# A two-layer graph network: two edits in the hand-written order of the first two groups (norm sums, and two statistics of the next x)

## The chip, the cores and the metric

The kernel runs on one core of one Trainium2 chip. The metric is the device time of one execution in microseconds (us); lower is better. Engines are called by the names of the profile: PE (TensorE, matrix products), PEld (its weight loads), DVE (VectorE), ACT (ScalarE), POOL (GpSimd) and SP (which only issues transfers).

## The reference, cut to what matters

The input x is 128 batches of 128 x 512, float32; adj is 128 x 128.

```python
# layer 0
h = jnp.maximum(_layernorm(x, axis=-1), 0.0)
q, k, v = (einsum('bnd,ed->bne', h, W) for W in (Wq, Wk, Wv))
rel = adj.T[None] * einsum('bnd,bmd->bnm', q, k)
rel = rel / jnp.linalg.norm(rel, axis=2, keepdims=True)
x = x + einsum('bnm,bmd->bnd', rel, v)
# layer 1
h = jnp.maximum(_layernorm(x, axis=-1), 0.0)
q, k, v = h @ Wq + bq, h @ Wk + bk, h @ Wv + bv      # 8 heads of 64
scores = q k^T / sqrt(64) + where(adj == 0, -1e9, 0)
x = x + softmax(scores) v
```

## The kernel before, in words

The 128 batches are worked in 32 groups of four (G = 4). One group of a layer is a matrix of 512 x 512, so a projection is a 512 x 512 x 512 product. It is made by a scheme with seven block products instead of eight (`Product`, L206 to L266). Its methods P1 to P7 each issue eight matmuls on PE into one PSUM bank (called x, y or z) and then either copy the bank into a quarter of the result on ACT (P1, P4, P5, P6: L232 or L235) or add the bank to a quarter on DVE (P2, P3, P7: L248). The bank x is used four times in turn, by P1, P6, P7 and P4: P6, P7 and P4 go on adding to what is there. So P4 may write only when P7's addition has read the bank.

For layer 0, q and k are folded into one matrix (`G`, the product with the folded weights; its result is gT), and `V` is the value product, with result v. P2 adds to the quarter of batches 0 and 1 and columns 0 to 255, P3 to batches 0 and 1 and columns 256 to 511, P7 to batches 2 and 3 and columns 256 to 511; P4 gives batches 2 and 3, columns 0 to 255.

The steps of layer 0 around the change are:
- `stat(b)` (L285): mean and variance of batch b of x, two DVE instructions (L289, L290); `inv(i)` (L292): four small instructions, which turn the statistics of two batches into scale and shift. In layer 0 all four are on POOL, in layer 1 the first two on DVE.
- `hn(i)` normalizes two batches on ACT (L308) and sends them to DRAM in blocks; `rd(i)` fetches them back (L197, SP); `T(i)` turns them on DVE (L320) into half i of h. h in this turned form feeds the products. `sumA` and `sumB` (L363 to L368) are the sums of blocks that the products need.
- `R` (L391, PE): the scores; `mask_rel` (L400, DVE) multiplies them with adj and gives rel; `square` (L406, ACT) gives the squares sq.
- `norms` (L408): turns sq (L412), and sums it in one reduction (L415), three small copies (L419) and four small reductions (L422), nine instructions on DVE; then one power on POOL gives rn (L427).
- `O(b)` (L431, PE): rel times v for one batch; `xO(b)` (L437, DVE): x becomes x + rn times that. Its batch of v must be whole by then.

Layer 1 has the products Q, K and V, the scores `S` (L476), the masking and maximum per row (`mkA`, `mkB`: L546 and L549; `add_mask`, `mx`: L488 and L493), the exponentials on ACT (`exC`, `exD`, `ex`: L529 and L500), a turn of the weights through DRAM (`wr`, `wt`), and the product with v (`A`, L632).

All five engines run under a manual schedule: on each engine the instructions stand in the order in which the program issues them, and each engine takes its own from the front, waiting where an operand is not ready. That order is written out by hand as lists of steps, which `run` plays. A step is named by who and what: m is layer 0 of this group, l layer 1 of the group before, p of the one before that, f layer 0 of the group after, and n is layer 1 of this group. `FIRST` is played once, for group 0; `SECOND` once, for group 1; `ORDER` for groups 2 to 31; `LAST` at the end. A step such as m.V.P3 issues its PE and its DVE instructions both, and so fixes their place in two queues.

In `ORDER` the four statistics of f and the two inversions stand together ahead of m.V.P6, and m.norms stands directly behind m.square.

Of the kernel before, what the change touches and what calls it, by code (L numbers as in the profile page):

```python
# [21 lines left out]
def kernel(  # L22
# [350 lines left out]
    class Layer0(Layer):  # L373
        n = 0
# [64 lines left out]
    class Layer1(Layer):  # L439
        n = 1  # L440
# [230 lines left out]
    FIRST = """  # L671
        m.sumA m.sumB m.start f.stat0 f.stat1 f.inv0 m.G.P1 m.G.P2 f.stat2 f.stat3 f.inv1 w.sumw m.G.P5 f.hn0 f.rd0 m.G.P6
        w.scale m.G.P3 m.V.P1 f.hn1 f.rd1 w.sumv m.G.P7 m.V.P2 w.sumq m.G.P4 m.V.P5
        m.R m.mask_rel m.square f.T0 m.V.P6 m.V.P3 m.norms m.V.P7 m.O0 m.xO0 m.O1 m.xO1 n.stat0 n.stat1
        n.inv0 m.V.P4 n.hn0 n.rd0 f.T1 f.start f.G.P1 f.sumA m.O2 m.xO2 m.O3 m.xO3 n.stat2 n.stat3 n.inv1
        f.G.P5 f.sumB f.G.P6 n.hn1 n.rd1 f.G.P2 f.G.P3 f.G.P7 n.T0 f.G.P4 w.sumk n.T1 n.start
    """.split()
    SECOND = """
        l.Q.P1 l.sumA l.Q.P2 l.sumB l.K.P1 l.K.P2 l.Q.P5 l.Q.P6 l.sto0 l.sto1 f.load0 f.load1 l.Q.P3 l.K.P5 l.K.P6 l.Q.P7
        l.K.P3 l.K.P7 f.load2 f.load3 l.Q.P4 l.K.P4 m.V.P1 f.stat0 f.stat1 f.inv0  # L680
        m.V.P2 m.V.P6 m.R m.mask_rel m.square m.norms f.stat2 f.stat3 f.inv1
        l.S0 l.S1 l.mkA1 m.V.P5 l.exC1 l.mkB1 m.V.P7 l.exD1 l.wr1 l.add_mask0 m.V.P3 l.mx0
        m.V.P4 l.ex0 l.wr0 m.O0 m.xO0 m.O1 m.xO1 n.stat0 n.stat1 n.inv0 n.hn0 n.rd0 l.start_v l.V.P1 m.O2 m.xO2 m.O3 m.xO3
        n.stat2 n.stat3 n.inv1 l.V.P2 l.V.P5 n.hn1 n.rd1 l.wt1 l.V.P6
# [33 lines left out]
    with tc.manual_schedule(engines={EN.PE, EN.SP, EN.Pool, EN.DVE, EN.Activation}):  # L718
        o, p, l, m = None, None, None, Layer0(0)
# [9 lines left out]
        f = Layer0(1)  # L729
# [3 lines left out]
        for g in range(NG):  # L733
            n = Layer1(g)
            if g:
                f = Layer0(g + 1) if g + 1 < NG else None
            run((FIRST, SECOND, ORDER)[min(g, 2)], o=o, p=p, l=l, m=m, n=n, f=f, w=Weights1())
            o, p, l, m = p, l, n, f
# [31 lines left out]
```

## Time and profile before

| | us |
|---|---|
| median of three runs | 2467.14 |
| the three runs | 2465.93 to 2468.3 |
| the profiled execution, its own time | 2463.63 |
| its span, first to last instruction | 2461.8 |
| PE busy | 2449.3 |
| DVE busy | 1756.1 |
| ACT busy | 1014.5 |
| POOL busy | 377.0 |

The granted TensorE clock was 0.999 on average. The chain of work that ended last lists stretches in order of time; in the stretch behind group 1 it goes from one PE step to the next. Times within the span are counted from its start: group 0's scores R run from about 39 to 43 us, those of group 1 from 97 to 101 us, and a later group takes about 76 us. A timeline row gives start, duration, engine, line, operation, the tiles it writes and reads, and, where the engine was idle before it, for how long and what ended that. A row of the waits gives the total, the number and the longest.

### The profile page before, as it was taken

How to read it: one execution, taken by the hardware profiler on the slowest of the kernel's cores; microseconds unless marked ns; L12 is line 12 of the kernel's file. 1: busy time of each engine (PE TensorE's matmuls, PEld its weight loads, DVE VectorE, ACT ScalarE, POOL GpSimd, SP SyncE). 2: the span in 40 equal slices, each digit the busy share in tenths (PEclk: the TensorE clock that was granted, in tenths of full speed). 3: DMA queues.
4: the chain of work that ended last, by engine and by line, in shares of the span. 5: the costliest groups of instructions: out<-in, count | busy, mean ns of one | idle time of the engine just before them, and what ended most of it. 6: DMA issues, size and time to landing. Idle time of an engine off the chain costs nothing.

```text
span 2461.8 us, 40194 instructions
## 1 busy us (share of the span) xinstructions
PE 2449.3 (99%) x14432; PEld 2111.2 (86%) x14432; DVE 1756.1 (71%) x2994; ACT 1014.5 (41%) x3248; POOL 377.0 (15%) x692
## 2 busy tenths in 40 slices
PE   9999999999999999999999999999999999999998
PEld 7888888888888888888888888888888888888887
DVE  6567776677767677776777667776767776677767
ACT  3334433444434344343443344443434434344434
POOL 5110111111111111111011111111111111111111
PEclk9999999999999999999999999999999999999999
DMA  5357656677566775566766667756677566676656
GB/s 189 99 164 206 178 166 178 172 204 198 161 174 171 189 214 161 163 182 180 206 178 170 175 171 204 196 162 174 172 190 213 162 170 174 180 205 186 165 156 163
DMA packets 396407, 438.18 MB, mean 178 GB/s; under 512 B 31600, under 2 KB 289008, under 8 KB 396208
## 3 DMA queue, kind: packets, MB, share of 16 engines
q1 hardware_dynamic: 297376, 201.22, 32.7%
q10 hardware_dynamic: 70000, 165.96, 18.2%
q0 software_dynamic: 28832, 68.44, 13.5%
q8 instruction: 114, 1.87, 0.3%
q14 instruction: 85, 0.70, 0.1%
HBM read 204.80 MB, written 230.69 MB: 177 GB/s over the span
## 4 chain that ended last, share of the span: by engine, by line
PE 96%; DVE 2%; DMA 1%; issue 0%; SPq 0%; POOL 0%; ACT 0%; DVEq 0%; POOLq 0%
PE pv_x L224 17%; PE pg_x L224 9%; PE pk_x L224 9%; PE pq_x L224 9%; PE pv_z L224 9%; PE pr L391 5%; PE po L632 5%; PE pq_z L224 5%; PE pg_z L224 5%; PE pk_z L224 4%; PE pv_y L224 4%; PE po L431 4%; PE pss L476 3%; PE pg_y L224 2%; PE pso L476 2%; PE pq_y L224 2%
## 5 line engine op out<-in xcount | busy, mean ns | idle before, releaser
L320 DVE STREAM_TRANSPOSE h<-u_h 128x1024 f32<-128x1024 f32 x126 | 156.6, 1243 | 215.7 <-DMA u_h<-d_h 214.9
L224 PE MATMUL pv_x<-wc_v,h 128*128 128x256 f32 x1280 | 306.1, 382 | 3.7 <-DVE v L248 2.7
L224 PEld LDWEIGHTS pv_x<-wc_v,h 128*128 128x128 f32 x1280 | 240.2, 190 | 55.3 <-issue 21.6
L666 POOL DMA_DIRECT2D out_dram<-o x124 | 110.7, 900 | 982.8 <-DVE o L659 939.2
L308 ACT ACTIVATE hn<-xb,shift,rstd 128x512 f32<-128x512 f32 x252 | 191.2, 807 | 149.7 <-POOL shift L300 122.1
L224 PE MATMUL pv_z<-wc_v,s 128*128 128x256 f32 x1024 | 245.2, 382 | 0.8 <-DVE v L241 0.8
L224 PEld LDWEIGHTS pv_z<-wc_v,s 128*128 128x128 f32 x1024 | 191.9, 190 | 29.8 <-DVE v L241 1.2
L232 ACT COPY gT<-pg_x 128x512 f32<-128x512 f32 x96 | 56.3, 586 | 364.0 <-PE pg_x L224 363.1
L224 PE MATMUL pq_x<-h,wc_q 128*128 128x256 f32 x768 | 181.6, 379 | 0.4 <-DVE h L320 0.2
L529 ACT ACTIVATE e<-pso,nmax 128x128 f32<-128x128 f32 x504 | 179.6, 393 | 5.5 <-DVE nmax L549 5.4
L224 PE MATMUL pv_x<-wc_v,s 128*128 128x256 f32 x768 | 181.5, 379 | 0.0
L224 PE MATMUL pk_x<-h,wc_k 128*128 128x256 f32 x768 | 181.5, 379 | 0.0
L289 DVE BATCH_NORM_STATS2 st<-xb 128x6 f32<-128x512 f32 x256 | 171.4, 669 | 8.2 <-DMA xb<-in_x_dram 8.1
L515 DVE STREAM_TRANSPOSE wT<-u_w 128x1024 f32<-128x1024 f32 x126 | 152.4, 1210 | 32.8 <-DMA u_w<-d_w 32.2
L224 PEld LDWEIGHTS pq_x<-h,wc_q 128*128 128x128 f32 x768 | 145.7, 190 | 20.9 <-PE pv_x L224 1.1
L224 PEld LDWEIGHTS pk_x<-h,wc_k 128*128 128x128 f32 x768 | 145.8, 190 | 20.0 <-issue 0.2
L224 PEld LDWEIGHTS pv_x<-wc_v,s 128*128 128x128 f32 x768 | 145.8, 190 | 19.9
L643 ACT COPY oT<-po 128x512 f32<-128x512 f32 x124 | 72.1, 582 | 206.3 <-PE po L632 203.9
L299 POOL TENSOR_TENSOR rstd<-rstd,mhalf 128x2 f32<-128x2 f32 x128 | 91.0, 711 | 408.0 <-DVE shift L298 408.0
L70 POOL DMA_DIRECT2D xb<-in_x_dram x124 | 69.0, 557 | 436.6 <-DMA out_dram<-xb 246.2
L232 ACT COPY v<-pv_x 128x512 f32<-128x512 f32 x96 | 56.3, 586 | 178.7 <-PE pv_x L224 178.7
L224 PE MATMUL pg_z<-s,wc_a 128*128 128x256 f32 x512 | 121.3, 380 | 0.8 <-ACT v L232 0.6
(153 smaller groups left out, 4906.0 us busy)
## 6 DMA issues: line engine op xcount, KB each, us to landing
d_h<-hn ACTq DMA_DIRECT2D x126, 512.0 KB, 3.8
u_h<-d_h SPq DMA_DIRECT2D x504, 128.0 KB, 3.7
d_w<-e ACTq DMA_DIRECT2D x126, 512.0 KB, 3.3
u_w<-d_w SPq DMA_DIRECT2D x504, 128.0 KB, 3.3
out_dram<-xb SPq DMA_DIRECT2D x126, 256.0 KB, 3.9
xb<-in_x_dram POOLq DMA_DIRECT2D x124, 256.0 KB, 4.7
d_o<-oT ACTq DMA_DIRECT2D x62, 512.0 KB, 2.8
u_o<-d_o SPq DMA_DIRECT2D x248, 128.0 KB, 4.0
```

The lines of the kernel that those rows point to most:

```text
L224: nc.tensor.matmul(ps[:, m, :], lhsT=lhsT, rhs=rhs, start=first and m == 0 and k == 0, stop=k == 1, skip_group_check=True,)
L232: nc.scalar.copy(to, ps)
L289: nc.vector.bn_stats(st, x_tiles[g, b])
L308: nc.scalar.activation(hn[:, r], x_tiles[g, b].rearrange("p (k j q) -> p j k q", j=TB, q=BK), AF.Relu, bias=self.shift[:, b : b + 1], scal ...
L320: nc.vector.transpose(half.rearrange("p k (t i) -> p t k i", i=BK), self.u.pop(i).rearrange("p t (k q) -> p t k q", q=BK),)
L391: nc.tensor.matmul(pr[:, b, :], lhsT=self.turned(k, b), rhs=self.gT[k // 2][:, k % 2, ts(b, P)], start=(k == 0), stop=(k == KD - 1),)
L431: nc.tensor.matmul(po, lhsT=self.rel[:, b, :], rhs=self.v[:, b, :], start=True, stop=True)
L476: nc.tensor.matmul(half[r][:, k, :], lhsT=self.qT[rows, k, ts(b, P)], rhs=self.kT[rows, k, ts(b, P)], start=True, stop=True,)
L515: nc.vector.transpose(self.wT[b].rearrange("p h (t i) -> p t h i", i=BK), self.uw.pop(b).rearrange("p t (h q) -> p t h q", q=BK),)
L529: nc.scalar.activation(e[:, :, i, :], sc[:, k, :].rearrange("p (j q) -> p j q", q=BK), AF.Exp, bias=nmax[:, i : i + 1], accum_out=self.tot ...
L632: nc.tensor.matmul(po[r * HD : (r + 1) * HD, k, :], lhsT=self.v[b // 2][:, b % 2, ts(2 * k + r, HD)], rhs=wT[:, r * NH + k, :], start=True ...
L666: nc.gpsimd.dma_start(out[g * G + b], o.rearrange("p k t q -> p (k t q)"), accum_op=ALU.add)
```

## The change

Two places in the written order. In `FIRST`, m.norms moves from behind m.V.P3 to behind f.T0, ahead of m.V.P6 and m.V.P3. In `SECOND`, f.stat2, f.stat3 and f.inv1 move from behind m.norms to ahead of m.V.P6, and with that ahead of m.R, m.mask_rel, m.square and m.norms. No step is added or taken away, and the lists `ORDER` and `LAST` stay as they are.

```diff
     FIRST = """
...
-        m.R m.mask_rel m.square f.T0 m.V.P6 m.V.P3 m.norms m.V.P7 m.O0 m.xO0 m.O1 m.xO1 n.stat0 n.stat1
+        m.R m.mask_rel m.square f.T0 m.norms m.V.P6 m.V.P3 m.V.P7 m.O0 m.xO0 m.O1 m.xO1 n.stat0 n.stat1
...
     SECOND = """
...
         l.K.P3 l.K.P7 f.load2 f.load3 l.Q.P4 l.K.P4 m.V.P1 f.stat0 f.stat1 f.inv0
-        m.V.P2 m.V.P6 m.R m.mask_rel m.square m.norms f.stat2 f.stat3 f.inv1
+        m.V.P2 f.stat2 f.stat3 f.inv1 m.V.P6 m.R m.mask_rel m.square m.norms
         l.S0 l.S1 l.mkA1 m.V.P5 l.exC1 l.mkB1 m.V.P7 l.exD1 l.wr1 l.add_mask0 m.V.P3 l.mx0
```

## The prediction

> **What bounds the kernel now.** I read the page first: busy shares, then the shares of the chain that ended last.
>
> ```profile
> span 2461.8 us, 40194 instructions
> ...
> PE 2449.3 (99%) x14432; PEld 2111.2 (86%) x14432; DVE 1756.1 (71%) x2994; ACT 1014.5 (41%) x3248; POOL 377.0 (15%) x692
> ...
> PE 96%; DVE 2%; DMA 1%; issue 0%; SPq 0%; POOL 0%; ACT 0%; DVEq 0%; POOLq 0%
> ```
>
> TensorE (PE) is busy for all but 2461.8 - 2449.3 = 12.5 us, and 96% of the chain is PE. An edit to another engine's order can only win time by removing a place where PE stands still. The next view is therefore who waited for whom, for PE alone (total, times, longest):
>
> ```profile
> PE pv_x L224 <- DVE v L248: 2.7, 2, 1.8
> ...
> PE pq_x L224 <- DVE h L320: 0.2, 1, 0.2
> ```
>
> The largest entry is two waits of V's product for L248, the DVE addition of a finished product into the tile v. They lie in the two groups that the diff touches. PE's timeline shows the first (start, us, engine, line, tiles, idle before it):
>
> ```profile
> 44.41 1.89 PE L224 MATMUL pv_z<-wc_v,s 128*128 128x256 f32 x8
> 46.13 1.89 PE L224 MATMUL pv_x<-wc_v,s 128*128 128x256 f32 x8
> 47.86 1.88 PE L431 MATMUL po<-v,rel 128*128 128x512 f32 x4
> 50.61 1.96 PE L224 MATMUL pv_x<-wc_v,h 128*128 128x256 f32 x8 [0.87 <-DVE v L248]
> ```
>
> These are V.P3, V.P7, O0 with O1, and V.P4. V.P4 writes into the bank that V.P7's addition reads, so it waits for that addition. DVE's timeline of the same time says why the addition was late:
>
> ```profile
> 43.49 1.23 DVE L320 STREAM_TRANSPOSE h<-u_h 128x1024 f32<-128x1024 f32 x1
> 46.40 0.69 DVE L248 TENSOR_TENSOR v<-pv_z,v 128x512 f32<-128x512 f32 x1 [1.68 <-PE pv_z L224]
> 47.01 0.70 DVE L412 STREAM_TRANSPOSE sqt<-sq 128x512 f32<-128x512 f32 x1
> ...
> 49.77 0.69 DVE L248 TENSOR_TENSOR v<-pv_x,v 128x512 f32<-128x512 f32 x1
> ```
>
> V.P7's addition could have run at about 48.12 (V.P3's starts 46.40 - 44.41 = 1.99 after its matmuls, and 46.13 + 1.99 = 48.12), but the norm sums (47.01 to 49.77) stood ahead of it. Before 46.40 DVE was idle for 1.68 us, although the squares (ACT, 43.60 + 0.63) were ready at 44.23. The second group, DVE and then PE:
>
> ```profile
> 104.95 0.69 DVE L289 BATCH_NORM_STATS2 st<-xb 128x6 f32<-128x512 f32 x1
> ...
> 106.58 0.67 DVE L546 TENSOR_TENSOR pso<-pso,mask 128x512 f32<-128x512 f32 x1
> ...
> 109.22 0.68 DVE L248 TENSOR_TENSOR v<-pv_x,v 128x512 f32<-128x512 f32 x1
> ```
> ```profile
> 106.23 1.89 PE L224 MATMUL pv_z<-wc_v,s 128*128 128x256 f32 x8
> 109.96 1.99 PE L224 MATMUL pv_x<-wc_v,h 128*128 128x256 f32 x8 [1.84 <-DVE v L248]
> ```
>
> From 102.19 on DVE has no gap until V.P7's addition at 109.22, and two statistics of the next x lie in that run (104.95 to 106.58, 1.63 us). Ahead of it, between 96.26 and 100.80, DVE is idle.
>
> **What these places cost.** I count from start to start, since the ends of matmuls are modelled. One product step takes 1.73 us where nothing waits, O0 with O1 1.72 (115.46 to 117.18 in the chain). Group 0: 47.86 to 50.61 is 2.75, so 1.03 too long, and V.P4 behind it takes 1.80, 0.07 too long. A second wait follows: O2 with O3 starts at 54.13, G.P5 at 56.16, which is 2.03, 0.31 too long, and the product behind it 1.83, 0.10 too long; the chain has sumA (L363, 55.41 to 56.10) just before it, itself at the end of an unbroken DVE run from xO0 on. Together 1.51 us. Group 1: 106.23 to 109.96 is 3.73, 2.00 too long, and 0.10 behind it: 2.10 us.
>
> **Part 1, group 0.** Nothing is added or removed; nine DVE instructions move ahead of one (V.P3's addition) and POOL's rn starts earlier. The order built from the changed code has PE, ACT and SP as before; no DMA is moved.
> - The norms start behind the transpose f.T0. An independent instruction starts 1.16 after such a transpose (65.70 to 66.86), so at 43.49 + 1.16 = 44.65. They take 2.76 (47.01 to 49.77): V.P3's addition starts at 47.41 instead of 46.40, and ends at 48.10.
> - This is the new wait. O0 reads the half of v that V.P3's addition writes; PE would be there at 47.86 and starts 0.06 after the addition's end (as at 109.90 to 109.96): 48.16. Late by 0.30, and some 0.08 behind it. Behind O0 on PE stand O1 and everything else.
> - V.P7's addition follows at about 48.1 and ends at 48.8. V.P4 is due at 48.16 + 1.72 + 0.07 = 49.95 and waits no longer.
> - rn (POOL, 1.01) ends at about 48.5. xO0 needs O0, 1.19 after its start (111.79 to 112.98): 49.35 instead of 50.86. The second follows at 50.15 and the statistics at about 50.8 instead of 52.19, 1.37 earlier. The run behind moves with them: sumA ends at 54.73. G.P5 is due at 49.95 + 3 x 1.73 = 55.13 (V.P4, G.P1, O2 with O3): the 0.31 goes too.
> - Next late is G.P4 at 65.84 behind G.P7's own addition (65.10); it hangs on PE alone and stays. n.T0's last landing (63.89, start 65.70) leaves 1.8 us, Q.P5 behind n.T1 has 1.9 us (72.59 to 74.58).
>
> Gain 1.51 - 0.38 = **1.13 us**. Bounds: 0.63, if the wait at G.P5 stays (0.41) and the hand-over takes 0.15 as at 50.46 to 50.61; 1.51, if O0 did not wait at all.
>
> POOL's rn comes beside V.P3's and V.P7's additions. Today it stands beside V.P7's (49.82 and 49.77), which takes 0.69 as elsewhere; but DVE L90 takes 1.75 beside POOL L90 (39.31 and 38.81), against 0.69 at 21.41 with POOL only issuing DMAs. I take nothing. The Trainium skill, "SBUF — State Buffer", section "Who interferes with whom", says that DVE and GpSimd share ports which the first holds for its whole instruction, but not against a DVE instruction with a single SBUF input, as these additions have; the trace agrees. If the lock held here all the same, V.P7's addition would come some 1 us later, at about 49.1, and the sum would lose 0.1 at most, an estimate by that page.
>
> **Part 2, group 1.** Four DVE instructions (two statistics of 0.69 and 0.66, two aggregations of 0.18) move from 104.95 to behind V.P2's addition, 96.3 to 97.9, in the 4.54 us in which DVE waits for the scores R. Their x landed at 78.3. POOL's four small instructions (inv1) move with them into idle time, ahead of rn. V.P7's addition starts at 109.22 - 1.63 = 107.59; its matmuls (104.51 + 1.99) and the scores (PE, 101.69 + 1.06) are ready. V.P4 starts at 108.33 instead of 109.96; free of waits it would be 107.96, so 0.37 stays. V.P3's addition and the exponentials keep their distance and move up alike; ACT and the transfers d_w, u_w, d_h, u_h follow. Gain **1.63 us**. Upper bound 2.10, the whole wait; lower bound 0.53: that is how far ahead n.T0 (ends 130.93) is of Q.P1 (131.46), and if its data did not come earlier, the rest would be given back there.
>
> **Sum.** 1.13 + 1.63 = 2.76 us. The profiled execution took 2463.63 us (span 2461.8): 2460.9 after. It lies 3.5 us below the median of the runs, 2467.14, from which 2464.4 follows. That is my forecast: 0.11%, less than the 0.2% (4.9 us) that I take as what a measurement of this kernel can tell from no change.
>
> **Rivals.**
> 1. *One gain is given back*: n.T0 does not move up with PE (group 1 yields 0.53), or group 0 only 0.63. For it: 281.67 and following show PE held at Q.P1 by a transpose that waited for its DMA, 283.06 - 280.92 = 2.14 against 1.83. Against: in both groups what feeds the transfers hangs on O0 to O3, which move up. Time: 2467.14 - 1.16 = 2466.0.
> 2. *Slower*: the later groups meet their transfers differently. Place: the boundary of groups, where n.T0 waits for u_h. In two of the 30 later groups PE loses there today, 0.31 at 283.06 and 0.30 at 290.35, and alike at 1116.64 and 1123.93: 0.61 a group. With five more such groups the gain is gone (2.76 / 0.61 = 4.5), and with the 28 others all hit the time is 2464.4 + 17.1 = 2481.5. Against: 76 us a group is PE's own pace, the transfers are released by work behind PE, and so they should shift as one.
> 3. *More than the stalls' length*, if PE ran slowly behind a gap. By rows: 16 matmuls (two steps, 3.46 us) at half speed behind each of the two long gaps would add 6.9 us, so 2457.5. Against: behind 50.90 and 110.28 the matmuls follow at 0.216 as anywhere, and the granted clock of both stretches is 1.00. The Trainium skill, "TensorE: Matmul & The Clock Gate", section "What's actually happening", gives such a halving after an idle window of about 3.4 us; the gaps here are shorter, and the trace agrees.
>
> That the change does not do what it says is ruled out by the built order.
>
> **Numbers.** Forecast 0.84, rival 1 0.10, rival 2 0.04, rival 3 0.02. The profiled execution shows that one can fall 3.5 us below the median, so 0.05 of the forecast lies below 2462.2. Faster by over 0.2%: 0.05 + 0.02 = 0.07; within: 0.79 + 0.10 = 0.89; slower: 0.04. Range: the profiled execution's own sum, 2460.9, is the low end; the high end is the smallest gain (1.16) with the runs' spread upward (1.2) and some room for rival 2: 2467.8.
>
> **What would show it.** Right: no wait of V.P4 in group 0, a new one of about 0.3 of po (L431) for L248; in group 1 a wait of about 0.2 instead of 1.84; PE's busy time unchanged and the span 2.8 shorter, with everything behind 131 earlier by 2.8. Wrong: G.P5 still late, Q.P1 waiting for L320, or steps of over 1.83 us at later boundaries.

## The result, and the profile after

| | before | after |
|---|---|---|
| median, 17 runs each | 2467.14 us | 2462.55 us |
| lowest to highest | 2464.55 to 2470.38 | 2460.41 to 2466.47 |
| ratio after to before | | 0.9984, 95% interval 0.9977 to 0.9991 |
| profiled execution, own time | 2463.63 | 2460.41 |
| its span | 2461.8 | 2458.6 |

The changed kernel is faster by 0.16%, and the interval (2.2 to 5.7 us) excludes no change. The forecast, 2.76 us less, lies in it. The medians lie 4.6 us apart, so the measured one is 1.9 us below 2464.4. With 17 runs each, this settles a change smaller than the 0.2% that the prediction took as the limit.

The page after, the same rows:

```profile
span 2458.6 us, 40193 instructions
...
PE 2450.2 (100%) x14432; PEld 2111.9 (86%) x14432; DVE 1756.6 (71%) x2994; ACT 1012.7 (41%) x3248; POOL 375.9 (15%) x692
...
PE 92%; DVE 4%; DMA 2%; issue 1%; SPq 0%; ACT 0%; POOL 0%; DVEq 0%; ACTq 0%; POOLq 0%
```

No engine's work changed (PE busy 2449.3 and 2450.2); PE's idle time went from 12.5 to 8.4 us. The waits of PE:

```profile
PE idle L121 <- POOL ident masks.py:199: 1.4, 1, 1.4
PE pg_x L224 <- DVE gT L248: 0.8, 1, 0.8
PE pv_x L224 <- DVE v L241: 0.5, 1, 0.5
PE pq_x L224 <- DVE h L320: 0.3, 2, 0.2
```

The entry of 2.7 us for V's product and L248 is gone. PE in group 0 (V.P6, V.P3, V.P7, O0 with O1, V.P4, G.P1, O2 with O3, and the first half of G.P5):

```profile
43.80 1.89 PE L224 MATMUL pv_x<-wc_v,s 128*128 128x256 f32 x8
45.52 1.89 PE L224 MATMUL pv_z<-wc_v,s 128*128 128x256 f32 x8
47.25 1.89 PE L224 MATMUL pv_x<-wc_v,s 128*128 128x256 f32 x8
49.23 1.98 PE L431 MATMUL po<-v,rel 128*128 128x512 f32 x4
51.05 1.89 PE L224 MATMUL pv_x<-wc_v,h 128*128 128x256 f32 x8
52.78 1.89 PE L224 MATMUL pg_x<-h,wc_a 128*128 128x256 f32 x8
54.51 1.88 PE L431 MATMUL po<-v,rel 128*128 128x512 f32 x4
56.22 1.03 PE L224 MATMUL pg_z<-s,wc_a 128*128 128x256 f32 x4
```

This execution happens to be 1.12 us late already at V.P6 (43.80 against 42.68; in the kernels below, equal up to here, the same step starts anywhere from 42.81 to 44.15), so steps must be read as differences. O0 now comes 1.98 after V.P7 instead of 1.73: the new wait, 0.25 us, which the list of waits does not have because the modelled end of V.P7's matmuls (47.25 + 1.89) covers most of it. V.P4 comes 1.82 after O0 instead of 2.75, and the row has no idle time any more. G.P5 comes 1.71 after O2 with O3 instead of 2.03. DVE shows the reason (T0, the first of the norms, V.P3's addition, V.P7's addition, xO):

```profile
44.60 1.24 DVE L320 STREAM_TRANSPOSE h<-u_h 128x1024 f32<-128x1024 f32 x1
45.76 0.67 DVE L412 STREAM_TRANSPOSE sqt<-sq 128x512 f32<-128x512 f32 x1
...
48.48 0.69 DVE L248 TENSOR_TENSOR v<-pv_z,v 128x512 f32<-128x512 f32 x1
49.18 0.69 DVE L248 TENSOR_TENSOR v<-pv_x,v 128x512 f32<-128x512 f32 x1
50.47 1.53 DVE L437 SCALAR_TENSOR_TENSOR xb<-po,rn,xb 128x512 f32<-128x512 f32 x2 [0.60 <-PE po L431]
```

The norms follow T0 after 1.16 and take 2.72. V.P3's addition ends at 49.17 and O0 starts 0.06 later. In group 1, DVE's first row below is V.P2's addition, then come the two statistics in what was idle time, and the run of masks and maxima no longer holds them; the second fence is PE's V.P5, and behind V.P7 its V.P3, V.P4 and O0:

```profile
95.53 0.69 DVE L248 TENSOR_TENSOR v<-pv_y,v 128x512 f32<-128x512 f32 x1 [4.67 <-PE pv_y L224]
96.14 0.68 DVE L289 BATCH_NORM_STATS2 st<-xb 128x6 f32<-128x512 f32 x1
...
100.76 0.69 DVE L400 TENSOR_TENSOR rel<-pr,adj_sb 128x512 f32<-128x512 f32 x1 [2.92 <-PE pr L391]
...
107.46 0.68 DVE L248 TENSOR_TENSOR v<-pv_x,v 128x512 f32<-128x512 f32 x1
```
```profile
102.63 1.99 PE L224 MATMUL pv_z<-wc_v,s 128*128 128x256 f32 x8
...
106.19 1.89 PE L224 MATMUL pv_z<-wc_v,s 128*128 128x256 f32 x8
108.19 1.99 PE L224 MATMUL pv_x<-wc_v,h 128*128 128x256 f32 x8
110.02 1.94 PE L431 MATMUL po<-v,rel 128*128 128x512 f32 x4
```

V.P4 comes 2.00 after V.P3, was 3.73. DVE's idle time ahead of the scores shrank from 4.54 to 2.92, by the 1.62 that the statistics take.

To compare executions I take two lengths from PE's starts: group 0 from V.P6 to Q.P1, and group 1 from V.P5 to O0. In the kernel before, these four steps are:

```profile
42.68 1.89 PE L224 MATMUL pv_x<-wc_v,s 128*128 128x256 f32 x8
67.67 1.89 PE L224 MATMUL pq_x<-h,wc_q 128*128 128x256 f32 x8
102.67 1.99 PE L224 MATMUL pv_z<-wc_v,s 128*128 128x256 f32 x8
111.79 1.95 PE L431 MATMUL po<-v,rel 128*128 128x512 f32 x4
```

Before: 67.67 - 42.68 = 24.99 and 111.79 - 102.67 = 9.12. After: 67.63 - 43.80 = 23.83 and 110.02 - 102.63 = 7.39. That is **1.16 + 1.73 = 2.89 us**, against a forecast of 1.13 + 1.63 = 2.76.

The spans differ by 3.2. That is the 2.89, less the 1.12 at the start, less 0.15 in the groups between, plus 1.6 in the tail, the last 27 us from its V.P5 on (26.66 against 25.06). There the bias addition of layer 1's V (L241, on DVE) stands behind a transpose that waited 2.06 us for its transfer u_o before and 0.45 after. So it is partly luck that this execution, at 2460.41, comes so near the 2460.9 that was worked out for it. The medians differ by 4.6. So the open question was whether later groups and the tail also wait less because of the change (theory B), or whether all of the gain is the 2.9 us and the rest is scatter (theory A).

### The profile page after: what moved, and what is told of

The parts are those of the page before. It is cut to its first block, busy times and chain, and to the rows that moved or that the text cites. A ratio compares the mean times of both kernels' runs of the same rounds, so it can differ in the third digit from the quotient of the medians.

```text
span 2458.6 us, 40193 instructions
## 1 busy us (share of the span) xinstructions
PE 2450.2 (100%) x14432; PEld 2111.9 (86%) x14432; DVE 1756.6 (71%) x2994; ACT 1012.7 (41%) x3248; POOL 375.9 (15%) x692
## 4 chain that ended last, share of the span: by engine, by line
PE 92%; DVE 4%; DMA 2%; issue 1%; SPq 0%; ACT 0%; POOL 0%; DVEq 0%; ACTq 0%; POOLq 0%
PE pv_x L224 16%; PE pg_x L224 9%; PE pq_x L224 9%; PE pk_x L224 8%; PE pv_z L224 8%; PE pq_z L224 5%; PE pr L391 5%; PE pk_z L224 4%; PE po L632 4%; PE pg_z L224 4%; PE po L431 4%; PE pv_y L224 4%; PE pss L476 3%; PE pg_y L224 2%; PE pso L476 2%; PE pk_y L224 2%
## 5 line engine op out<-in xcount | busy, mean ns | idle before, releaser
L224 PE MATMUL pq_z<-s,wc_q 128*128 128x256 f32 x512 | 121.5, 380 | 0.7
```

Source lines behind the costliest of these rows:

```text
L224: nc.tensor.matmul(ps[:, m, :], lhsT=lhsT, rhs=rhs, start=first and m == 0 and k == 0, stop=k == 1, skip_group_check=True,)
```

## The experiments

Eleven kernels ran, in three sessions; each ratio is against the kernel before on the same chip, whose median was 2474.15 (e0 to e3), 2467.57 (e4 to e7) and 2474.26 us (e8 to e10). "Later waits" is the sum over PE's steps from 135 to 2390 us that start over 0.16 us too late. The step Q.P1 of group 1, at about 130 us, which waits for a transfer through n.T0, lies in none of the three columns.

| kernel | group 0 | group 1 | later waits | ratio to before, interval |
|---|---|---|---|---|
| before (first profile) | 24.99 | 9.12 | 2.7 | |
| after (first profile) | 23.83 | 7.39 | 2.7 | 0.9984 (0.9977 to 0.9991) |
| e0, same as before | 25.00 | 9.12 | 11.4 | 1.0004 (0.9995 to 1.0013) |
| e1, first group only | 23.84 | 9.12 | 12.3 | 0.9993 (0.9985 to 1.0002) |
| e2, second group only | 24.99 | 7.39 | 12.4 | 0.9995 (0.9986 to 1.0004) |
| e3, both again | 23.84 | 7.40 | 7.6 | 0.9988 (0.9979 to 0.9996) |
| e4, T0 behind V.P3 | 23.65 | 7.39 | 3.1 | 0.9983 (0.9974 to 0.9992) |
| e5, sumk ahead of V.P3 | 27.77 | 7.39 | 7.3 | 0.9997 (0.9989 to 1.0006) |
| e6, V.P7 ahead of mkB1 | 23.64 | 7.72 | 5.9 | 0.9987 (0.9978 to 0.9996) |
| e7, mkB3 ahead of wt1 too | 23.65 | 7.72 | 4.5 | 0.9985 (0.9976 to 0.9994) |
| e8, e5 again (one run) | 26.38 | 7.39 | 7.9 | |
| e9, two sums ahead (one run) | 25.17 | 7.39 | 11.9 | |
| e10, V.P3 too ahead | 23.65 | 7.01 | 13.3 | 0.9982 (0.9973 to 0.9991) |

**e0: nothing changed.**

> Nothing is changed: the kernel before, as a measure of what two runs of one program differ by. Theory A (the gain is the length of PE's removed waits in groups 0 and 1, and all that lies behind 131 us moves as one): time within 1.5 us of the kernel before, the waits in the first two groups as before (O0/O1 to V.P4 1.03 too long, G.P5 0.31, V.P4 of group 1 2.00), and the waits behind 131 us and in the tail (0.96 and 1.17 in the one profile of before) another sum, by a us or two. Theory B (the changed order shifts the phase of the transfers, and the later groups and the tail wait less for it): the later waits as in the first profile of before, within some 0.3 us.

The first two groups repeat to 0.01 us. The later waits do not: 11.4 us against 2.7 (the 0.96 of the expectation is another count of that first profile), far more than either theory allowed for, with the time 7 us higher on this chip for the kernel before itself. PE's waits in it, to be held against those of before:

```profile
PE pv_x L224 <- DVE v L248: 2.7, 2, 1.8
PE pq_x L224 <- DVE h L320: 2.7, 5, 0.8
PE pg_z L224 <- DVE s L363: 2.5, 5, 0.9
```

The first row is the two waits of the first groups, unchanged. The others are Q.P1 at the boundary of groups and G.P5 behind the sums of a new h; in both h comes from a transfer. This execution's span is 11.5 us longer than that of the first profile, and 10.5 of them come in between 135 and 2390 us: the later groups explain the difference between executions and sessions better than any edit here. Q.P1 of group 1 is late too, with nothing changed: it comes 20.24 us after O0, where it was 19.67.

**e1 and e2: one part alone.**

```diff
 e1, FIRST:   ... m.square f.T0 [m.norms] m.V.P6 m.V.P3 m.V.P7 m.O0 ...      (SECOND as before)
 e2, SECOND:  m.V.P2 [f.stat2 f.stat3 f.inv1] m.V.P6 m.R ... m.norms         (FIRST as before)
```

> Only the edit in FIRST (norms ahead of V.P6 and V.P3 in group 0). Theory A: 1.1 to 1.2 us less than before; O0 late by 0.25 to 0.30, V.P4 and G.P5 on time, group 1's V.P4 still 2.0 late. Theory B: of the 4.6 us between the medians most is got already by shifting what follows, so 2 us or more.

> Only the edit in SECOND (two statistics and inv1 ahead of V.P6 in group 1). Theory A: 1.6 to 1.8 us less than before; group 0's waits as before (1.5 in all), V.P4 of group 1 late by 0.27 to 0.37. The two parts add up to the whole. Theory B: 2.5 us or more, and the sum of the two parts is not the whole.

By the lengths each part gives its own gain and none of the other's: 1.15 and 1.73. By the medians 2.5 and 1.6 us less, with intervals of about 4 us that each include no change at all. The second group's V.P4 in e1 and in e2:

```profile
105.21 1.89 PE L224 MATMUL pv_z<-wc_v,s 128*128 128x256 f32 x8
108.94 1.99 PE L224 MATMUL pv_x<-wc_v,h 128*128 128x256 f32 x8 [1.84 <-DVE v L248]
```
```profile
106.77 1.89 PE L224 MATMUL pv_z<-wc_v,s 128*128 128x256 f32 x8
108.77 1.99 PE L224 MATMUL pv_x<-wc_v,h 128*128 128x256 f32 x8
```

**e3: both again.**

> The changed kernel once more, on the same chip as the two halves. Theory A: 2.8 to 2.9 us less than before in the first 131 us, and a time 2.8 us less, give or take the 1 us of the medians; waits behind 131 us of the same size as in the unchanged kernel. Theory B: 4 to 5 us less, with later waits and tail smaller in both profiles of this kernel than in both of the kernel before.

Against e0 the two lengths are 1.16 and 1.72 shorter, and the medians differ by 3.1 us (0.9988, 0.9979 to 0.9996). Theory B expected fewer later waits wherever the change is made. On this chip alone it looks so: 7.6 us in e3, against 11.4, 12.3 and 12.4 without both edits. But this one execution (2467.66 us) was 3.4 us faster than the median of its own kernel, and e8, e9 and e10, which have both edits and ran on a chip with the same median for the kernel before, have 7.9, 11.9 and 13.3. In the first pair the waits are equal (2.7 and 2.7). The tail is 26.66, 26.39, 26.23 and 26.23 us without both edits, 25.06 and 26.22 in the changed kernel, and 26.61 and 25.09 in e4 and e6, which have the same LAST: it is short or long without an edit. So nothing speaks clearly for B; that the change does nothing at all behind 131 us is not shown, since an effect of 1 us would be lost in this scatter.

**e4: T0 between V.P3 and V.P7.**

```diff
-        m.R m.mask_rel m.square f.T0 m.norms m.V.P6 m.V.P3 m.V.P7 m.O0
+        m.R m.mask_rel m.square m.norms m.V.P6 m.V.P3 f.T0 m.V.P7 m.O0
```

> The changed kernel with f.T0 moved from ahead of the norms to between V.P3 and V.P7 in group 0. Theory A (V.P3's addition behind the norms sets O0): the norms start when the squares are there, 0.4 earlier, V.P3's addition ends by about 47.7 and O0 (47.86) no longer waits; V.P7's addition ends 0.1 ahead of V.P4; G.P5 still on time by 0.1. 0.35 us less than the changed kernel by the timeline, not to be seen in the time. Rival: O0's wait is for something else (po's bank, rn), and stays at 0.25, or the transpose, now behind, makes V.P4 or G.P5 late by 0.5.

PE in group 0 (V.P7, O0 with O1, V.P4):

```profile
47.60 1.89 PE L224 MATMUL pv_x<-wc_v,s 128*128 128x256 f32 x8
49.33 1.98 PE L431 MATMUL po<-v,rel 128*128 128x512 f32 x4
51.14 1.96 PE L224 MATMUL pv_x<-wc_v,h 128*128 128x256 f32 x8
```

O0 is on time (1.73), so V.P3's addition was what it waited for. V.P4 comes after 1.81 instead of 1.72: the transpose in between takes that from V.P7's addition, and G.P1, the product behind V.P4, comes 0.07 late (1.80). The gain over the changed kernel is 0.19, not 0.35.

**e5, e8 and e9: the price of a late V.P3 addition.** All three delay it by DVE work that has its place elsewhere.

```diff
 e5, e8:  m.square f.T0 m.norms +w.sumk m.V.P6 m.V.P3 ...        f.G.P4 -w.sumk n.T1
 e9:      the first two of sumk's four sums there, the other two at the old place
```

> The changed kernel with the four sums of K's weights (DVE, 0.65 each, 2.6 us in all) moved from the end of FIRST to between the norms and V.P3 in group 0: the price of a late V.P3 addition. Theory A: O0 late by 0.25 + 2.6 = 2.85, one us for one us, nothing won back at the old place; the time 2.6 us more than the changed kernel, about that of the kernel before. Rival: part of the delay is taken up by the waits behind it (G.P4's 0.95 among them), and less than 1.9 us is lost.

O0 is 2.79 late, as expected (2.85), and nothing is won back. But group 0 is 3.94 us longer than in the changed kernel, not 2.6. In e5, O0 with O1, then V.P4:

```profile
51.98 3.39 PE L431 MATMUL po<-v,rel 128*128 128x512 f32 x4 [2.62 <-DVE v L248]
55.20 1.89 PE L224 MATMUL pv_x<-wc_v,h 128*128 128x256 f32 x8
```

Four matmuls that take 1.72 from start to start take 3.22 here. The table by stretches has the granted clock after POOL's column:

```profile
52.00:55.20 3.20, 3.20 (x4) 1.42 (x5) 1.27 (x2) 0.00 (x0) 0.00 (x0) 0.56 0.02 5
```

So behind a gap of 2.62 us the clock was halved for most of this stretch. e8 repeats the kernel, to see whether the gap's length alone decides.

> The kernel with the sums of K's weights ahead of V.P3 in group 0 once more. In its first profile PE stood still for 2.62 us before O0, and the four matmuls of O0 and O1 behind it took 3.23 us instead of 1.73 at a granted clock of 0.56. Theory C: the clock halves behind any such gap, so O0 and O1 take about 3.2 us again. Theory D: it depends on where the gap falls in a window that the program does not set, so this profile may show 1.7 to 1.8 us and a clock of 1.00.

The same two views in e8:

```profile
52.09 1.98 PE L431 MATMUL po<-v,rel 128*128 128x512 f32 x4 [2.63 <-DVE v L248]
53.91 1.89 PE L224 MATMUL pv_x<-wc_v,h 128*128 128x256 f32 x8
```
```profile
52.00:55.20 3.20, 3.10 (x10) 2.01 (x11) 2.47 (x5) 0.00 (x0) 0.00 (x0) 1.00 0.00 0
```

The same gap, and full clock, so theory C is out. Whether a gap of 2.6 us is punished depends on something that the program does not set.

The traces' records of the granted clock say what that may be. In each of the thirteen profiles the first record of full clock begins at another time, from 4.37 to 7.34 us, and every later change comes a whole number of periods of 3.413 us after it. In e5 a period ends at 51.43, with PE busy for 1.33 us of it; there the clock halves, for one period. In e8 a period ends at 51.06, in the middle of the gap: PE is busy for 1.82 us of the period before and 2.38 of the one behind, and the clock stays. In the kernel before, the whole gap of group 1 lies in one period (106.77 to 110.18, PE busy for 1.57), and the clock stays too. This fits theory D. Three periods give no limit, and busy time alone is no rule: at the end of the kernel before, 2.33 us of PE's work in a period (2455.14 to 2458.55) was followed by the half clock.

> Half the dose: two of the four sums of K's weights (1.3 us) stand between the norms and V.P3 in group 0, the other two at the old place. One us for one us: O0 late by 0.25 + 1.3 = 1.55; V.P4 and G.P5 on time behind it. A gap of about 1.4 us is shorter than the 1.84 of the kernel before, behind which the clock stayed at 1.00: O0 and O1 take 1.8 us, and group 0 is 1.3 us longer than in the changed kernel, not 3.9 as with all four sums.

O0 is 1.58 late, O0 with O1 take 1.82, and group 0 is 1.34 longer than in the changed kernel: 1.3 us for 1.3 us of work. Together with e8 (2.55 longer for 2.54 of work) the price is one for one.

**e6 and e10: the 0.27 that is left in group 1.**

```diff
 e6, SECOND:   l.exC1 +m.V.P7 l.mkB1 -m.V.P7 l.exD1 l.wr1 l.add_mask0 m.V.P3 l.mx0       (on e4)
 e10, SECOND:  l.exC1 +m.V.P7 l.mkB1 -m.V.P7 l.exD1 l.wr1 +m.V.P3 l.add_mask0 -m.V.P3 l.mx0  (on e4)
```

> As the one with f.T0 behind V.P3, and in SECOND V.P7 stands ahead of l.mkB1, so that its addition does not queue behind a mask and a maximum (1.33 us). Theory A: V.P4 of group 1 is no longer late (0.27 and 0.10 gained), exD1 on ACT starts 0.7 later and nobody waits for it; 0.7 us less than the changed kernel by the timeline. Rival: the later exponentials delay the transfer of the weights, and wt1 or A0 is late by up to 0.7.

V.P4 is on time (106.74 - 105.01 = 1.73), but group 1 is 0.33 longer: V.P7's addition now waits 0.26 for its matmuls with the rest of DVE's queue behind it, and V.P3's addition, last in that queue, holds O0.

```profile
106.74 1.89 PE L224 MATMUL pv_x<-wc_v,h 128*128 128x256 f32 x8
109.18 1.95 PE L431 MATMUL po<-v,rel 128*128 128x512 f32 x4 [0.55 <-DVE v L248]
```

> As the one with f.T0 behind V.P3, and in SECOND V.P7 ahead of l.mkB1 and V.P3 ahead of l.add_mask0, so that neither addition queues behind layer 1's masks. Theory A: V.P4 and O0 of group 1 both on time: from V.P5 to O0's start 6.9 us instead of 7.39, 0.4 to 0.5 us less than the one it starts from by the timeline; in the time not to be told from it, 3 to 3.5 us less than before. Rival: add_mask0 and the maxima come later, xO0 with them, and n.T0 is late at Q.P1 (131) by what was gained.

With both additions ahead, V.P7, V.P3, V.P4 and O0 follow each other after 1.73: with the 1.83 from V.P5 to V.P7 that is 7.01. But xO0 starts 1.75 after O0 instead of 1.20, since the mask and the maxima now stand ahead of it, and Q.P1 is late by 0.41 at 128.84 in this one profile, where n.T0 had 0.53 to spare before. That is what the rival expected, but it is not shown: n.T0 starts 18.62 us after O0, against 17.68 in the changed kernel; xO0 explains 0.55 of these 0.94, and in e0 n.T0 started 18.85 after O0 with nothing changed. The time (0.9982) is not to be told from that of the change or of e4.

**e7: the end.**

```diff
-        l.V.P7 l.wt0 l.tw2 l.wt1 l.mkB3 l.exB3 l.V.P4        (LAST, on e6)
+        l.V.P7 l.wt0 l.tw2 l.mkB3 l.exB3 l.wt1 l.V.P4
```

> As the one before, and in LAST l.mkB3 and l.exB3 stand ahead of l.wt1, whose transpose waits for a transfer. Theory A: the last exponentials start about 1.2 us earlier, the last transposes on PE then wait for the products An0 and An1 alone; 0.3 to 0.5 us less at the end. Rival: wt1 and with it An1 come later by as much, and nothing is won or up to 1 us lost.

The rival took place: the transpose of wt1 starts 1.07 us later than in e6 (2449.90 against 2448.83), and An1 now waits 0.21 us for it. The tail took 25.54 us against 25.09 in e6, and the ratio is the same within the intervals: nothing won that could be seen. The tail says little by itself: with one and the same LAST it took from 25.1 to 26.8 us.

No version is measurably faster than the changed kernel; e4 and e10 are shorter by 0.2 and 0.6 us in the first two groups alone.

## Why the prediction was right

- *Group 0, 1.13.* 1.16 measured. V.P4's wait went, the wait at G.P5 went, and O0's new wait is 0.25 with 0.10 behind it, where 0.30 and 0.08 were expected: that is where the 0.03 lie. The norms started 1.16 after T0 and V.P3's addition released O0 after 0.06, both as taken from other rows. e4 shows that this addition is the cause, e5, e8 and e9 that it is paid one for one.
- *Group 1, 1.63.* 1.73 measured. The term that was a little small is the distance by which V.P7's addition moves: from V.P5 to it 6.55 before (109.22 - 102.67) and 4.83 after (107.46 - 102.63), so 1.72. The statistics took 1.63, and the mask behind the norms' last sums starts 0.10 sooner behind them (104.81 - 104.16 = 0.65) than the statistics did (104.95 - 104.20 = 0.75); why, no run shows.
- *G.P4's wait stays*: 0.94 in both profiles. *POOL's rn beside the additions*: rn runs from 48.53 to 49.54 and both additions take 0.69, as taken.
- *The signs.* Both waits that were named are there, 0.25 and 0.27, but in the distances from start to start and not in the list of waits. "Everything behind 131 earlier by 2.8" did not come out in this profile: Q.P1 of group 1 starts at 129.69 instead of 131.46, 1.77 earlier, since the execution began 1.12 late.
- *Rival 1 (given back).* Q.P1 of group 1 comes 19.67 us after O0 in both profiles, so nothing was given back there. How near the rival was is a matter of the execution: Q.P1 was 0.57 late in e0, with nothing changed, 0.37 in e2 and 0.41 in e10. The spare time of 0.53 that the prediction read from one profile is not a fixed size.
- *Rival 2 (later groups wait more).* Not seen. But its price stood on one profile, with 2.7 us of later waits; e0 has 11.4 without any edit. What was taken as "two of 30 groups" is a matter of the session, and the difference is larger than the change itself.
- *Rival 3 (slow clock behind a gap).* The gaps of 0.87 and 1.84 us cost their own length and 0.07 and 0.10 behind it, no more. The reason given, a window of 3.4 us that the gap must fill, does not hold: in e5 a gap of 2.62 us was enough once.
- *From the sum to the median.* 2.9 us of the 4.6 lie in the first two groups. The interval begins at 2.2, and the kernels that keep both edits and add no work, e3, e4, e6, e7 and e10, gave 3.1, 3.2, 2.5, 3.1 and 4.3. For the other 1.7 us of the first result no cause is shown; scatter of the later groups is the likely one.

## What to carry to other kernels

Where an engine takes its instructions in a fixed order, the question for each is what it can do in the time in which its next operand is not ready: the nine instructions of the norms and the four of the statistics cost 2.9 us more where they stood ahead of an addition that PE needed than in such holes. Look past the addition that is late today to the one that the move makes late: here it was paid one for one. An effect of 0.1% is settled by start-to-start lengths in the timeline, which repeated to 0.01 us, while the times of one kernel spread over 6 us. That holds for stretches in which nobody waits for a transfer; Q.P1, just behind the second length, moved by up to 0.57 us.

## What the runs showed of the hardware

After one idle gap of 2.62 us PE's clock was granted at one half (0.56 over the next 3.2 us, four matmuls 1.5 us longer); after a gap of 2.63 us in the same program it stayed at 1.00. A gap of 1.42 us (e9) and the gap of 1.84 us (before, e0, e1) were not followed by it. The clock changed only at multiples of 3.413 us after its first record. The Trainium skill, "TensorE: Matmul & The Clock Gate", section "What's actually happening", describes a free-running window of 3413 ns; the traces agree, with the period of 3.413 us, but a gap of three quarters of its length (2.62 us, e5) was enough for the slow clock.
